# Tokenizer and first attention of a vision tower: the order of all engines written by hand

## The chip, the cores and the metric

The kernel runs on one core of one Trainium2 chip. The metric is the device time of one execution in microseconds (us). A core has a matrix engine (TensorE, PE in the profile), three engines for elementwise work (VectorE or DVE, ScalarE or ACT, GpSimd or POOL), and SyncE (SP), whose queue issues most of the transfers. Each engine has a queue of its own, and the engines wait for each other through semaphores.

## The reference

32 images of 3 x 256 x 256 become 256 tokens of width 256 each, and pass two layers. All arithmetic is in float32. The part that the change touches is the tokenizer, the first attention and the start of the first FFN:

```
h = patches @ W.T + b                                 # tokenizer
xn = layernorm(h) / max(norm(layernorm(h)) / 16, 1e-5) * g
uv = silu(xn @ W_uv + b_uv)                           # u 512, v 512, base 128 columns
q, k = base * gamma[0] + beta[0], base * gamma[1] + beta[1]
attn = square(relu(q @ k.T / sqrt(128)))
h = h + (u * (attn @ v)) @ W_o + b_o
y = layernorm(h);  weights = y @ wr + br              # FFN: the best 127 of 256 tokens of an image
sel = the 127 tokens of greatest weight
h = h + y;  h[sel] += weights[sel] * (gelu(sel @ w1 + b1) @ w2 + b2)
```

The second layer (an attention by phases, and a gated FFN with heads and experts) is computed after that and is not changed in its order.

## The kernel before, in words

The residual `H` stays on chip for all 32 images: two chunks of 128 tokens by 256 columns each. The work goes in stages: A, the tokenizer, one image at a time; B, the first attention, two images (a pair) at a time; C, the FFN with token choice, four images (a quad) at a time; then the second layer. Line numbers are those of the kernel before unless said otherwise. All matmuls are recorded by the helper `mm` (L114), transposes by their own lines (L187 for activations, L349 for weights of tokens, L240 for chosen tokens), the add of an image's patches by L303, statistics by `stats` (L122 and L123), the normalisation by `normed` (L173).

**Stage A**, `unit_a`: for each image 12 matmuls of 128 x 256 from patches that SP loads up to five images ahead, one add of the bias into `H` on VectorE, and the statistics of both chunks. After each second image `factors_b` makes the scale of the next normalisation: four small operations on GpSimd (two powers among them) and two on VectorE (L327, L328). PE, ACT and SP follow the written order here, VectorE and GpSimd an order that the scheduler chose.

**Stage B**, `unit_b`, in a pipeline of pairs, in whose newest stage a pair is normed (`bx`, L173), turned (`transposed`: eight transposes into two banks, of which ACT copies the first at L192 and VectorE the second at L194), and its `base` is made (two matmuls of 128 x 512, Silu on ACT at L392) with queries and keys `bq`, `bk` on VectorE (L394, L396). A step later the pair has its scores with relu (ACT, L405) and square (GpSimd, L407), its gates `uT` (eight matmuls, L415) and its values `bv` (eight matmuls, an add on VectorE at L422, Silu on ACT at L423). Another step later come the products of attention and values, gated on VectorE into `gT` (L439), and the output with `w_wo`, whose result VectorE adds to `H` (L452) before it takes the statistics for stage C and GpSimd makes their power. `b_o` is added to `H` by GpSimd (L382).

Two further steps belong to stage C: `norm_c` norms the images of the pair (`cx`) and makes the weights of tokens `cw` (L341, with a sum as a second result); `ranks` calls `rank_c` for both images. `rank_c` has two transposes of `cw` into half of a bank which both images share, then four comparisons on VectorE (L354 and L356, twice each), three small operations, and two indirect stores on GpSimd (L365), which write the normed tokens to memory in their order of rank. In stage B the scheduler orders all engines: `phase` only says in which order the parts are handed to it.

**Stage C** is in written order on all engines already. It begins with the ranks of the last two pairs, and then has hidden layer, output and fetch of each quad. The second layer is ordered by the scheduler.

Of the kernel before, what the change touches and what calls it, by code (L numbers as in the profile page):

```python
# [32 lines left out]
F32 = mybir.dt.float32  # L33
# [6 lines left out]
P = 128  # L40
# [38 lines left out]
def vit_tower(tc, a, out):  # L79
# [115 lines left out]

    def one_step(active):
        return [g for g in active if next(g, g) is not g]

    def phase(unit, images, steps):

        active = []
        for b in range(0, B, images):
            active = one_step([unit(b)] + active)
        for _ in range(steps - 1):
            active = one_step(active)
        return active


    region, passing_x = ExitStack(), ExitStack()
# [33 lines left out]

    patches = a["patches"].rearrange("(k p) t -> p k t", p=P)
    with (
        tc.tile_pool(name="a_w", bufs=1) as pw,
        tc.tile_pool(name="a_x", bufs=6) as pp,  # L250
        tc.manual_schedule(engines={ENG.PE, ENG.Activation, ENG.SP}),
    ):
# [33 lines left out]

        loaded = []
        st_b = new_stats("b")

        def unit_a(b):  # L290
            if b == 0:
                ps = [bank() for _ in range(NC)]
                for k in range(n_k):
                    for c in range(NC):
                        mm(ps[c][:, 0:D], x0[k][:, c * P : (c + 1) * P], tokW[k], k == 0, k == n_k - 1)
                for c in range(NC):
                    nc.vector.tensor_tensor(H[b][:, c, :], ps[c][:, 0:D], row_a("tok_b"), ALU.add)
            else:
                x, p = xs_a.pop(b), bank()
                for c in range(NC):  # L300
                    for k in range(n_k):
                        mm(p[:, c * D : (c + 1) * D], x[:, k, c * P : (c + 1) * P], tokW[k], k == 0, k == n_k - 1)
                nc.vector.tensor_tensor(  # L303
                    H[b], p.rearrange("p (c d) -> p c d", c=NC), over(row_a("tok_b"), [P, NC, D], 1), ALU.add
                )
                if b + 5 < B:
                    load_patches(b + 5)
            st, _, i = at(st_b, b)
            for c in range(NC):
                stats(st, i, c, H[b][:, c, :])  # L310
            if b == 4:
                loaded.extend(layer_0_weights())
            if b % 2:
                factors_b(b - 1)
            yield

        def factors_b(b):


            st, rs, i = at(st_b, b)  # L320
            q = slice(i * NC, (i + 2) * NC)
            var = st.rearrange("p i c s -> p (i c) s")[:, q, 1]
            low = spool.tile([P, 2 * NC], F32, name="low")
            pow_rstd(low, var)
            nc.gpsimd.tensor_scalar(rs[:, q], var, 1e-36, 1.0, ALU.max, ALU.mult)
            nc.gpsimd.tensor_tensor(rs[:, q], rs[:, q], minus_half[:, 0 : 2 * NC], ALU.pow)
            nc.vector.scalar_tensor_tensor(rs[:, q], low, 1e5, rs[:, q], ALU.mult, ALU.min)  # L327
            nc.vector.tensor_scalar(rs[:, q], rs[:, q], col("attn_g"), None, ALU.mult)  # L328

        phase(unit_a, 1, 2)  # L330
        wuv, row_b, wo, row_c, before, w1 = loaded

    def norm_c(b):
        x = px.tile([P, NC, D], F32, name="cx", bufs=6)
        normed(x, b, st_c)
# [33 lines left out]
    with (  # L369
# [3 lines left out]
        st_c = new_stats("c")  # L373
        scale = 1.0 / math.sqrt(128.0)

        def unit_b(b0):
            xs = []
            for j in range(2):
                x = p4.tile([P, NC, D], F32, name="bx")
                normed(x, b0 + j, st_b)  # L380
                xs.append(x)
                nc.gpsimd.tensor_tensor(  # L382
                    H[b0 + j], H[b0 + j], over(row_b("b_o"), [P, NC, D], 1), ALU.add
                )
            xT = p2.tile([P, 2, 2 * N], F32, name="bxT")
            transposed(xT, xs, copy_split)

            base = p2.tile([P, 2 * N], F32, name="base")
            p = bank()
            for k in range(2):  # L390
                mm(p, wuv[:, k, 1024:1152], xT[:, k, :], k == 0, k == 1)
            nc.scalar.activation(base, p, AF.Silu, bias=col("b_base"))  # L392
            q = p2.tile([P, 2 * N], F32, name="bq")
            nc.vector.tensor_scalar(q, base, col("gamma", 0), col("beta", 0), ALU.mult, ALU.add)  # L394
            kk = p2.tile([P, 2 * N], F32, name="bk")
            nc.vector.tensor_scalar(kk, base, col("gamma", 1), col("beta", 1), ALU.mult, ALU.add)  # L396

            yield
            attn = []
            for j in range(2):  # L400
                p = bank()
                for m in range(NC):
                    mm(p[:, m * N : (m + 1) * N], kk[:, j * N + m * P : j * N + (m + 1) * P], q[:, j * N : (j + 1) * N])
                r = p2.tile([P, NC, N], F32, name="relu")
                nc.scalar.activation(r.rearrange("p m n -> p (m n)"), p, AF.Relu, scale=scale)  # L405
                t = p4.tile([P, NC, N], F32, name="attn")
                nc.gpsimd.tensor_tensor(t, r, r, ALU.mult)  # L407
                attn.append(t)

            uT = p2.tile([P, 4, 2 * N], F32, name="uT")  # L410
            for hc in range(4):
                p = bank()
                for k in range(2):
                    mm(p, wuv[:, k, hc * P : (hc + 1) * P], xT[:, k, :], k == 0, k == 1)
                nc.scalar.activation(uT[:, hc, :], p, AF.Silu, bias=col("b_u", hc))  # L415
            vs = []
            for tb in range(2 * NC):
                p = bank()
                for k in range(2):
                    mm(p, xT[:, k, tb * P : (tb + 1) * P], wuv[:, k, 512:1024], k == 0, k == 1)  # L420
                v = p4.tile([P, 512], F32, name="bv", bufs=8)
                nc.vector.tensor_tensor(v, p, row_b("b_v"), ALU.add)  # L422
                nc.scalar.activation(v, v, AF.Silu)  # L423
                vs.append(v)

            yield
            gTs = []
            for j in range(2):
                gT = p2.tile([P, 4, N], F32, name="gT")
                for half in range(2):  # L430
                    p = bank()
                    for h in range(2):
                        hc = 2 * half + h
                        for m in range(NC):
                            mm(
                                p[:, h * N : (h + 1) * N], vs[j * NC + m][:, hc * P : (hc + 1) * P],
                                attn[j][:, m, :], m == 0, m == NC - 1,
                            )
                    nc.vector.tensor_tensor(  # L439
                        gT[:, 2 * half : 2 * half + 2, :], p.rearrange("p (h n) -> p h n", h=2),  # L440
                        uT[:, 2 * half : 2 * half + 2, j * N : (j + 1) * N], ALU.mult,
                    )
                gTs.append(gT)
            if b0 == B - 2:
                turn_c(0, quads[0], 0)
            for j in range(2):
                b, gT = b0 + j, gTs[j]
                p = bank()
# [5 lines left out]
                for c in range(NC):  # L454
                    stats(st, i, c, H[b][:, c, :])

            pow_rstd_of(st_c, b0, 2)

            yield
            normed_c[b0] = [norm_c(b0 + j) for j in range(2)]  # L460

            yield
            ranks(b0)
            if b0 in (2, 6):
                first_ranks(b0 - 2, quads[b0 // 4], 0)

# [6 lines left out]


        phase(unit_b, 2, 3)
    region_b.close()

# [211 lines left out]
    with region_c:  # L689
# [20 lines left out]
        def fetch(b0, s, half):  # L710
            s.y = s.y if half else []
            for b in range(b0 + 2 * half, b0 + 2 * half + 2):
                y = px.tile([P, NC, D], F32, name="cx", bufs=6)
                for c in range(NC):
# [31 lines left out]
        preparing = prepare()  # L746
        with tc.manual_schedule(engines={ENG.PE, ENG.DVE, ENG.Activation, ENG.Pool, ENG.SP}):
            for t in range(END_C):
                if t < 2:
                    ranks(B - 4 + 2 * t)  # L750
                if t == 0:
                    normed_c[B - 2] = [norm_c(B - 2 + j) for j in range(2)]
                if t == END_C - 2:
                    norm_d(0, pairs[0], px, "cx", 6)
                step_c(t)
                if t >= 8:
                    next(preparing, None)
        passing.close()
    region.close()
    region_c0.close()  # L760


    st_e = new_stats("e")
    with (
# [45 lines left out]
        def values_d(b0, s):  # L810
            s.v = []
            for j in range(2):
                p = bank()
                for c in range(NC):
                    for k in range(2):
                        o = j * N + c * P
                        mm(p[:, c * D : (c + 1) * D], s.xT[:, k, o : o + P], wv[:, k, :], k == 0, k == 1)
                v = p8.tile([P, NC, D], F32, name="dv", bufs=6)
                nc.vector.tensor_tensor(
# [783 lines left out]
```

## Time and profile before

| | us |
|---|---|
| median of three runs | 2049.75 |
| lowest and highest run | 2048.95 and 2054.02 |
| the profiled execution, its own time | 2053.58 |
| span of the profiled execution | 2051.8 |
| end of stage A on TensorE in it (from the span's start) | 173.04 |
| end of the last output matmuls of stage B | 711.89 |

The profile has six parts: busy time of each engine, the span in 40 slices, the DMA queues, the chain of work that ended last, the costliest groups of instructions, and the transfers. Each row of the timeline is an instruction or several equal ones with their start, their length, and, in brackets, how long their engine sat idle before them and what ended that. A float32 matmul shows as two rows. The granted clock of TensorE stands in windows as a number from 0 to 1; its mean over the span is 0.977.

### The profile page before, as it was taken

What the parts mean: (1) busy time and instruction counts of PE and PEld (TensorE: products, weight loads), DVE (VectorE), ACT (ScalarE), POOL (GpSimd) and SP (SyncE); (2) the same over time, 40 slices, a digit from 0 to 9 for tenths busy, and PEclk for the clock granted to TensorE, in tenths of its full rate; (3) what the DMA queues carried; (4) which work ended last, traced back from release to release, by engine and by line L of the source; (5) the groups of instructions that cost most, each with busy time, mean ns of one, the idle gap of its engine ahead of it and who ended that gap; (6) DMA issues with size and microseconds to landing.
All of it is one profiled execution on the core that took longest, in us unless ns stands there. A gap on an engine that the chain in (4) does not pass through costs nothing.

```text
span 2051.8 us, 38271 instructions
## 1 busy us (share of the span) xinstructions
PE 1973.4 (96%) x15412; PEld 1431.7 (70%) x15412; DVE 1334.2 (65%) x3591; ACT 832.5 (41%) x1569; POOL 731.1 (36%) x691
## 2 busy tenths in 40 slices
PE   9998999999999899999999999999999999999983
PEld 8885676666667657666667677667777777777762
DVE  2335557667675634435655566547898989998986
ACT  0001322222221121222443444367777777777762
POOL 1224224334341443336432333103444444444443
PEclk9999999999999999999998999989999999999996
DMA  9540000000000222221000000001121212121212
GB/s 296 151 135 1 0 1 31 18 24 16 16 18 29 87 81 72 60 70 57 1 0 1 1 1 1 1 17 38 39 63 43 64 43 63 44 62 45 64 48 53
DMA packets 69687, 95.12 MB, mean 46 GB/s; under 512 B 8576, under 2 KB 50944, under 8 KB 69120
## 3 DMA queue, kind: packets, MB, share of 16 engines
q1 hardware_dynamic: 62784, 75.04, 13.1%
q0 software_dynamic: 6144, 16.79, 2.7%
q8 instruction: 123, 2.02, 0.4%
q10 hardware_dynamic: 576, 0.79, 0.1%
q14 instruction: 60, 0.49, 0.1%
HBM read 46.45 MB, written 20.97 MB: 33 GB/s over the span
## 4 chain that ended last, share of the span: by engine, by line
PE 90%; DVE 5%; DMA 1%; ACT 1%; issue 1%; POOL 1%; SPq 0%; DVEq 0%; ACTq 0%; POOLq 0%
PE bank L114 85%; PE bank L646 2%; PE bank L187 2%; PE bank L1148 1%; DMA both<-hx 1%; PE bank L349 1%; DVE bank L994 0%; ACT bxT L192 0%; DVE fout L1157 0%; PE bank L240 0%; DMA patch<-in_patches_dram 0%; DMA cx<-results,rank_of 0%; DVE six L122 0%; DVE two L1079 0%; DVE fout L1153 0%
## 5 line engine op out<-in xcount | busy, mean ns | idle before, releaser
L996 ACT ACTIVATE et<-bank 128x512 f32<-128x512 f32 x384 | 202.4, 598 | 59.0 <-DVE bank L994 58.3
L114 PEld LDWEIGHTS bank<-ev,et 128*64 128x64 f32 x6144 | 198.0, 137 | 33.8 <-ACT et L996 21.3
L994 DVE TENSOR_TENSOR bank<-bank,w_tri 128x256 f32<-128x256 f32 (+1 forms) x384 | 173.6, 514 | 69.6 <-PE bank L114 67.6
L114 PE MATMUL bank<-ev,et 128*64 128x74 f32 (+1 forms) x6144 | 210.9, 226 | 0.0
L1074 POOL TENSOR_TENSOR eo<-eo,gate 128x1024 f32<-128x1024 f32 x64 | 121.9, 1925 | 226.5 <-DVE gate L1071 207.9
L114 PE MATMUL bank<-g,sx 64*128 64x512 f32 (+1 forms) x512 | 192.7, 506 | 0.7 <-ACT g L954 0.7
L114 PE MATMUL bank<-g,sw 64*128 64x512 f32 (+1 forms) x512 | 191.8, 506 | 0.0
L114 PE MATMUL bank<-tokW,patch 128*128 128x256 f32 x768 | 166.7, 380 | 2.3 <-DMA patch<-in_patches_dram 2.3
L114 PEld LDWEIGHTS bank<-tokW,patch 128*128 128x128 f32 x768 | 146.1, 190 | 23.0 <-issue 2.7
L114 PE MATMUL bank<-bxT,w_wuv 128*128 128x512 f32 x320 | 149.2, 605 | 5.5 <-ACT bxT L192 3.9
L192 ACT COPY bxT<-bank 128x512 f32<-128x512 f32 x16 | 9.4, 586 | 342.6 <-PE bank L187 342.6
L1026 POOL TENSOR_TENSOR hv<-hv,minus_half 128x8 f32<-128x8 f32 x64 | 119.5, 1867 | 5.3
L1012 ACT COPY eo<-bank 128x286 f32<-128x286 f32 x256 | 97.2, 421 | 58.3 <-PE bank L114 51.8
L114 PE MATMUL bank<-xsel,w_w 128*128 128x512 f32 x256 | 113.3, 600 | 0.0
L114 PE MATMUL bank<-attn,bv 128*128 128x256 f32 x512 | 113.3, 379 | 0.0
L114 PE MATMUL bank<-w_wo,gT 128*128 128x256 f32 x512 | 113.1, 379 | 0.0
L114 PE MATMUL bank<-w_w,hT 128*128 128x256 f32 x512 | 113.1, 379 | 0.0
L114 PE MATMUL bank<-w_wuv,bxT 128*128 128x512 f32 x256 | 112.5, 592 | 0.0
L114 PEld LDWEIGHTS bank<-attn,bv 128*128 128x128 f32 x512 | 97.1, 190 | 19.5 <-issue 6.9
L114 PEld LDWEIGHTS bank<-w_w,hT 128*128 128x128 f32 x512 | 96.7, 190 | 15.8 <-issue 3.3
L114 PEld LDWEIGHTS bank<-w_wo,gT 128*128 128x128 f32 x512 | 97.2, 190 | 13.2
L114 PEld LDWEIGHTS bank<-bxT,w_wuv 128*128 128x128 f32 x320 | 59.8, 192 | 66.3 <-issue 53.0
(245 smaller groups left out, 3980.2 us busy)
## 6 DMA issues: line engine op xcount, KB each, us to landing
patch<-in_patches_dram SPq DMA_DIRECT2D x31, 768.0 KB, 4.7
sw<-sx SPq DMA_DIRECT2D x64, 128.0 KB, 2.4
both<-fxT SPq DMA_DIRECT2D x64, 128.0 KB, 2.5
both<-hx SPq DMA_DIRECT2D x64, 128.0 KB, 2.3
out_dram<-fout SPq DMA_DIRECT2D x32, 256.0 KB, 2.5
cs<-ranked SPq DMA_DIRECT2D x32, 128.0 KB, 3.0
results<-cy SPq DMA_DIRECT2D x32, 128.0 KB, 1.7
w_w<-in_w_dram SPq DMA_DIRECT2D x2, 1024.0 KB, 10.2
```

The lines of the kernel that those rows point to most:

```text
L114: nc.tensor.matmul(o, lhsT, rhs, start=first, stop=last)
L187: nc.tensor.transpose(p[:, o : o + P], x[:, c, k * P : (k + 1) * P], ident)
L192: nc.scalar.copy(o, i)
L349: nc.tensor.transpose(pw[:, c * P : (c + 1) * P], w[:, c : c + 1].to_broadcast([P, P]), ident)
L646: nc.tensor.transpose(p[:, o : o + P], x[:, c, k * P : (k + 1) * P], ident)
L994: nc.vector.tensor_tensor(own, own, over(tri, [P, n_e, P], 1), ALU.add)
L996: nc.scalar.activation(t, p, AF.Exp)
L1012: nc.scalar.copy(im.o[:, c * NH + n, 0:OC], p[:, 0:OC])
L1026: nc.gpsimd.tensor_tensor(v, v, minus_half, ALU.pow)
L1074: nc.gpsimd.tensor_tensor(im.mix[k], im.mix[k], over(im.gate[:, :, 2 * k : 2 * k + 2], [P, NC * NH, 2, HD], 3), ALU.mult)
L1148: nc.tensor.transpose(im.po[:, o : o + P], im.fT[:, k, c * P : (c + 1) * P], ident)
```

## The change

From the start of stage A to the end of stage C one block, `by_hand`, now keeps the written order on PE, VectorE, ACT, GpSimd and SP; after it the scheduler works as before. The generators `unit_b` and `phase` are gone. Their parts are functions (`norm_b`, `turn_b`, `base_b`, `queries_b`, `scores_b`, `gates_b`, `values_b`, `gated_b`, `output_b`), which a loop over steps t calls in a written order. `ranks` stands between base and queries; the norm of the next pair is the last call of a step.

In stage A `factors_b` is split: `powers_b` on GpSimd after the odd image, the two operations on VectorE an image later. Pairs 0 and 1 are normed after images 26 and 28. Pair 0 is turned, and has its base, queries and keys, ahead of the last image; these lie in tiles (`xsel`, `cs`) of stage C which are not yet in use. Normed tokens of stage B now come from the pool `cx`, with 8 buffers where there were 6. `dv`, a tile of the second layer, has 4 buffers instead of 6.

```diff
-        tc.manual_schedule(engines={ENG.PE, ENG.Activation, ENG.SP}),
+    by_hand = ExitStack()
+    by_hand.enter_context(tc.manual_schedule(engines={ENG.PE, ENG.DVE, ENG.Activation, ENG.Pool, ENG.SP}))
...
+    def norm_b(b0, s):
+        s.xs = []
+        for j in range(2):
+            x = px.tile([P, NC, D], F32, name="cx", bufs=8)
+            normed(x, b0 + j, st_b)
+            s.xs.append(x)
+            h = H[b0 + j]
+            nc.gpsimd.tensor_tensor(h, h, over(row_b("b_o"), [P, NC, D], 1), ALU.add)
...
-        phase(unit_a, 1, 2)
+        for b in range(B):
+            if b == B - 1:
+                half = [p0.tile([P, 4, D], F32, name="cs", bufs=2).rearrange("p j d -> p (j d)") for _ in range(2)]
+                turn_b(0, pairs_b[0], p0, "xsel")
+                base_b(0, pairs_b[0], half[0][:, 0 : 2 * N])
+                queries_b(0, pairs_b[0], half[0][:, 2 * N :], half[1][:, 0 : 2 * N])
+            unit_a(b)
+            if b == 4:
+                wuv, row_b, wo, row_c, before, w1 = layer_0_weights()
+            if b % 2:
+                powers = powers_b(b - 1)
+            elif b:
+                factors_b(*powers)
+            if b in (B - 6, B - 4):
+                u = (b - B + 6) // 2
+                norm_b(2 * u, pairs_b[u])
...
-        phase(unit_b, 2, 3)
+        for t in range(B // 2 + 2):
+            def pair(u):
+                return (2 * u, pairs_b[u]) if 0 <= u < B // 2 else None
+
+            new, old, older = pair(t) if t else None, pair(t - 1), pair(t - 2)
+            if new:
+                turn_b(*new, p2, "bxT")
+                base_b(*new, p2.tile([P, 2 * N], F32, name="base"))
+            if t >= 4:
+                ranks(2 * (t - 4))
+                if t in (5, 7):
+                    first_ranks(2 * t - 10, quads[t // 2 - 2], 0)
+            if new:
+                queries_b(*new, p2.tile([P, 2 * N], F32, name="bq"), p2.tile([P, 2 * N], F32, name="bk"))
+            if old:
+                scores_b(*old)
+                gates_b(*old)
+                values_b(*old)
+            if t == 1:
+                factors_b(*powers)
+            if t >= 3:
+                normed_c[2 * (t - 3)] = [norm_c(2 * (t - 3) + j) for j in range(2)]
+            if older:
+                gated_b(*older)
+                if t == B // 2 + 1:
+                    turn_c(0, quads[0], 0)
+                output_b(*older)
+            if 2 <= t + 1 < B // 2:
+                norm_b(*pair(t + 1))
...
-                v = p8.tile([P, NC, D], F32, name="dv", bufs=6)
+                v = p8.tile([P, NC, D], F32, name="dv", bufs=4)
```

The other functions of the list hold the statements of `unit_b` unchanged.

More of the change, by code (lines that the diff above doesn't have):

```diff
@@ L194, in copy_split @@
             nc.vector.tensor_copy(o, i)
[L196 to L209, printed above, removed]
+    by_hand = ExitStack()
+    by_hand.enter_context(tc.manual_schedule(engines={ENG.PE, ENG.DVE, ENG.Activation, ENG.Pool, ENG.SP}))
     region, passing_x = ExitStack(), ExitStack()
@@ L247, in vit_tower, with turn_b, base_b, queries_b @@
     patches = a["patches"].rearrange("(k p) t -> p k t", p=P)
+    st_b, st_c = new_stats("b"), None
+    scale = 1.0 / math.sqrt(128.0)
+    class PairB:
+        pass
+    pairs_b = [PairB() for _ in range(B // 2)]
+    def norm_b(b0, s):
[6 more added lines that the diff above has]
+            nc.gpsimd.tensor_tensor(h, h, over(row_b("b_o"), [P, NC, D], 1), ALU.add)
+    def turn_b(b0, s, pool, name):
+        s.xT = pool.tile([P, 2, 2 * N], F32, name=name)
+        transposed(s.xT, s.xs, copy_split)
+    def base_b(b0, s, base):
+        s.base, p = base, bank()
+        for k in range(2):
+            mm(p, wuv[:, k, 1024:1152], s.xT[:, k, :], k == 0, k == 1)
+        nc.scalar.activation(base, p, AF.Silu, bias=col("b_base"))
+    def queries_b(b0, s, q, k):
+        s.q, s.k = q, k
+        nc.vector.tensor_scalar(q, s.base, col("gamma", 0), col("beta", 0), ALU.mult, ALU.add)
+        nc.vector.tensor_scalar(k, s.base, col("gamma", 1), col("beta", 1), ALU.mult, ALU.add)
     with (
@@ L285, in layer_0_weights @@
             )
-        loaded = []
-        st_b = new_stats("b")
         def unit_a(b):
@@ L310, in unit_a, with powers_b @@
                 stats(st, i, c, H[b][:, c, :])
[L311 to L317, printed above, removed]
+        def powers_b(b):
             st, rs, i = at(st_b, b)
@@ L326, in factors_b @@
             nc.gpsimd.tensor_tensor(rs[:, q], rs[:, q], minus_half[:, 0 : 2 * NC], ALU.pow)
-            nc.vector.scalar_tensor_tensor(rs[:, q], low, 1e5, rs[:, q], ALU.mult, ALU.min)
-            nc.vector.tensor_scalar(rs[:, q], rs[:, q], col("attn_g"), None, ALU.mult)
-        phase(unit_a, 1, 2)
-        wuv, row_b, wo, row_c, before, w1 = loaded
+            return rs[:, q], low
+        def factors_b(rs, low):
+            nc.vector.scalar_tensor_tensor(rs, low, 1e5, rs, ALU.mult, ALU.min)
+            nc.vector.tensor_scalar(rs, rs, col("attn_g"), None, ALU.mult)
+        for b in range(B):
[14 more added lines that the diff above has]
+                norm_b(2 * u, pairs_b[u])
     def norm_c(b):
-        x = px.tile([P, NC, D], F32, name="cx", bufs=6)
+        x = px.tile([P, NC, D], F32, name="cx", bufs=8)
         normed(x, b, st_c)
@@ L373, in vit_tower, with scores_b @@
         st_c = new_stats("c")
[L374 to L399, printed above, removed]
+        def scores_b(b0, s):
+            s.attn = []
             for j in range(2):
@@ L402, in unit_b @@
                 for m in range(NC):
-                    mm(p[:, m * N : (m + 1) * N], kk[:, j * N + m * P : j * N + (m + 1) * P], q[:, j * N : (j + 1) * N])
+                    o = j * N + m * P
+                    mm(p[:, m * N : (m + 1) * N], s.k[:, o : o + P], s.q[:, j * N : (j + 1) * N])
                 r = p2.tile([P, NC, N], F32, name="relu")
@@ L407, in unit_b, with gates_b @@
                 nc.gpsimd.tensor_tensor(t, r, r, ALU.mult)
-                attn.append(t)
-            uT = p2.tile([P, 4, 2 * N], F32, name="uT")
+                s.attn.append(t)
+        def gates_b(b0, s):
+            s.uT = p2.tile([P, 4, 2 * N], F32, name="uT")
             for hc in range(4):
@@ L413, in unit_b, with values_b @@
                 for k in range(2):
-                    mm(p, wuv[:, k, hc * P : (hc + 1) * P], xT[:, k, :], k == 0, k == 1)
-                nc.scalar.activation(uT[:, hc, :], p, AF.Silu, bias=col("b_u", hc))
-            vs = []
+                    mm(p, wuv[:, k, hc * P : (hc + 1) * P], s.xT[:, k, :], k == 0, k == 1)
+                nc.scalar.activation(s.uT[:, hc, :], p, AF.Silu, bias=col("b_u", hc))
+        def values_b(b0, s):
+            s.vs = []
             for tb in range(2 * NC):
@@ L419, in unit_b @@
                 for k in range(2):
-                    mm(p, xT[:, k, tb * P : (tb + 1) * P], wuv[:, k, 512:1024], k == 0, k == 1)
+                    mm(p, s.xT[:, k, tb * P : (tb + 1) * P], wuv[:, k, 512:1024], k == 0, k == 1)
                 v = p4.tile([P, 512], F32, name="bv", bufs=8)
@@ L423, in unit_b, with gated_b @@
                 nc.scalar.activation(v, v, AF.Silu)
-                vs.append(v)
-            yield
-            gTs = []
+                s.vs.append(v)
+        def gated_b(b0, s):
+            s.gTs = []
             for j in range(2):
@@ L435, in unit_b @@
                             mm(
-                                p[:, h * N : (h + 1) * N], vs[j * NC + m][:, hc * P : (hc + 1) * P],
-                                attn[j][:, m, :], m == 0, m == NC - 1,
+                                p[:, h * N : (h + 1) * N], s.vs[j * NC + m][:, hc * P : (hc + 1) * P],
+                                s.attn[j][:, m, :], m == 0, m == NC - 1,
                             )
@@ L440, in unit_b, with output_b @@
                         gT[:, 2 * half : 2 * half + 2, :], p.rearrange("p (h n) -> p h n", h=2),
-                        uT[:, 2 * half : 2 * half + 2, j * N : (j + 1) * N], ALU.mult,
+                        s.uT[:, 2 * half : 2 * half + 2, j * N : (j + 1) * N], ALU.mult,
                     )
-                gTs.append(gT)
-            if b0 == B - 2:
-                turn_c(0, quads[0], 0)
+                s.gTs.append(gT)
+        def output_b(b0, s):
             for j in range(2):
-                b, gT = b0 + j, gTs[j]
+                b, gT = b0 + j, s.gTs[j]
                 p = bank()
@@ L457, in unit_b @@
             pow_rstd_of(st_c, b0, 2)
[L459 to L465, printed above, removed]
         normed_c = {}
@@ L712, in fetch @@
             for b in range(b0 + 2 * half, b0 + 2 * half + 2):
-                y = px.tile([P, NC, D], F32, name="cx", bufs=6)
+                y = px.tile([P, NC, D], F32, name="cx", bufs=8)
                 for c in range(NC):
@@ L746, in vit_tower @@
         preparing = prepare()
[L747 to L757, printed above, removed]
+        for t in range(END_C):
+            if t < 2:
+                ranks(B - 4 + 2 * t)
+            if t == 0:
+                normed_c[B - 2] = [norm_c(B - 2 + j) for j in range(2)]
+            if t == END_C - 2:
+                norm_d(0, pairs[0], px, "cx", 8)
+            step_c(t)
+            if t >= 8:
+                next(preparing, None)
         passing.close()
@@ L760, in vit_tower @@
     region_c0.close()
+    by_hand.close()
     st_e = new_stats("e")
```

## The prediction

> **What bounds the kernel now.** I read the page first: busy shares and the chain that ended last.
>
> ```profile
> PE 1973.4 (96%) x15412; PEld 1431.7 (70%) x15412; DVE 1334.2 (65%) x3591; ACT 832.5 (41%) x1569; POOL 731.1 (36%) x691
> PE 90%; DVE 5%; DMA 1%; ACT 1%; issue 1%; POOL 1%; SPq 0%; DVEq 0%; ACTq 0%; POOLq 0%
> ```
>
> TensorE is the bound: 90% of the chain is its own work. The change can only win where TensorE idles, and loses wherever it makes TensorE wait. So I cut the time at the stage borders (columns: stretch, its length, busy us of PE, PEld, DVE, ACT, POOL, then the granted clock, DMA share, GB/s).
>
> ```profile
> 173.04:204.32 31.28, 25.73 (x64) 12.19 (x65) 19.19 (x32) 9.55 (x14) 15.66 (x14) 0.84 0.00 1
> 204.32:665.10 460.78, 457.01 (x1670) 302.54 (x1669) 293.50 (x718) 108.53 (x169) 158.58 (x148) 1.00 0.05 17
> 665.10:721.02 55.92, 47.04 (x193) 34.38 (x192) 39.66 (x129) 8.33 (x12) 22.64 (x25) 0.94 0.27 86
> ```
>
> The join from tokenizer to attention (first row) wastes TensorE at a clock of 0.84. The attention's steady part has 3.8 us of idle in 461 us at full clock: nothing is to be had there. The third row is the join to the FFN, which the change touches only at its edge. Next, one steady step on TensorE in the timeline (start, us, and the wait before it in brackets).
>
> ```profile
> 532.87 0.38 PE L349 MATMUL bank<-ident,cw 128*128 128x128 f32 x2
> 533.09 1.04 PE L187 MATMUL bank<-ident,bx 128*128 128x128 f32 x8
> 534.37 1.13 PE L114 MATMUL bank<-bxT,w_wuv 128*128 128x512 f32 x2 [0.24 <-ACT bxT L192]
> 535.33 1.46 PE L114 MATMUL bank<-bq,bk 128*128 128x256 f32 x6
> 536.62 1.02 PE L114 MATMUL bank<-bxT,w_wuv 128*128 128x512 f32 x2
> 537.68 0.43 PE L349 MATMUL bank<-ident,cw 128*128 128x128 f32 x2
> 565.93 0.38 PE L349 MATMUL bank<-ident,cw 128*128 128x128 f32 x2
> ```
>
> The step is 565.93 - 532.87 = 33.06 us. The scheduler put score matmuls (bq,bk) between the two base matmuls, and 4.6 us between the rank transposes of one image and of the other (L349): each wait for VectorE is filled with other matmuls.
>
> [...] Both images of a pair share one rank bank, so the second image's transposes wait until VectorE has read the first's; the trace has that wait at 2.15 to 4.46 us (below). [...] half clock for 10.2 us from 714.8 and 3.4 us from 977.7. [...] four norms took 1.41 us, but three beside a GpSimd add took 1.97.
>
> **The join A to B: a gain.** Before, TensorE went 31.28 us from the tokenizer's end to the next turn. Its work in there, at full-clock pitches: two turns of 8 transposes (16 x 0.109 = 1.7), four base matmuls of two rows (8 x 0.43 = 3.4), scores (8 x 0.216 = 1.7), gates and values (32 x 0.43 = 13.7): 20.6 us. Wasted: 10.7. After, pair 0 was normed at images 26 and 28, and its turn and base stand ahead of image 31. Waits that stay: ACT's copy of the first half (0.45); VectorE's copy of the second, queued behind image 30's add, statistics and factors (about 1.1); for pair 1, again 0.45, and 0.6 for its copy behind image 31's statistics. Sum 2.6. Gain 10.7 - 2.6 = 8.1, its slow clock included. The rest of the tokenizer is free: an image takes 5.2 us on TensorE, VectorE needs some 2.6 of it plus 1.4 for norms at two images, and the GpSimd powers (2.5) get a whole image's time.
>
> **The turn: a new wait, once a step.** In the changed program as built, VectorE's order at the end of a step is: add of the second image's output, its statistics, four norms of the *next* pair, and TensorE goes from the last output matmul straight to the transposes of those norms. Nothing is queued between them; behind the waiting transpose stand all matmuls of the next step. Count from X, the end of TensorE's issue of the output. Rows:
>
> ```profile
> 562.68 0.69 DVE L452 TENSOR_TENSOR h<-h,bank 128x512 f32<-128x512 f32 x1 [2.76 <-PE bank L114]
> 955.02 0.43 DVE L122 BATCH_NORM_STATS2 six<-h 128x6 f32<-128x256 f32 x1
> 955.48 0.18 DVE L123 BATCH_NORM_AGGREGATE st_d<-six 128x2 f32<-128x6 f32 x1
> 961.03 1.41 DVE L173 TENSOR_SCALAR dx<-h,st_d,rs_d 128x256 f32<-128x256 f32 x4 [0.64 <-DMA results<-cy]
> ```
>
> VectorE starts its add at X+0.20 (566.13 against 565.93 before). Add to statistics 0.73; two times (0.46 to the aggregate, 0.10 on): free at X+2.05. Norms 1.41: X+3.46. Fourth transpose 0.15 later, X+3.6; ACT copies from X+3.97 to 4.56, base starts X+4.6; VectorE's copy is done at about 5.2, before the second half needs it at 5.5; four rows of 0.43 end at X+6.33. GpSimd's `b_o` add stands behind its two rstd operations (0.2 and 1.04 us after the statistics), so it starts when the norms are nearly over and I give them no contention; if it hits, up to 1.0 more.
>
> **The ranks: a second wait in the same step.** They now come right after base, four transposes in a row; the second two wait for VectorE's four comparisons.
>
> ```profile
> 715.39 0.69 PE L349 MATMUL bank<-ident,cw 128*128 128x128 f32 x2 [2.90 <-DVE ctmp L356]
> 720.54 0.69 PE L349 MATMUL bank<-ident,cw 128*128 128x128 f32 x2 [4.46 <-DVE ctmp L356]
> 729.89 0.38 PE L349 MATMUL bank<-ident,cw 128*128 128x128 f32 x2
> 732.43 0.43 PE L349 MATMUL bank<-ident,cw 128*128 128x128 f32 x2 [2.15 <-DVE ctmp L356]
> ```
>
> The last pair is the clean case, VectorE being free: 732.43 - 729.89 = 2.54, and 0.27 to the next matmul. So the second image's transposes start at X+6.33+2.54 = 8.87 and scores at X+9.14. Scores 1.73, gates 6.87, values 6.87, gated 6.9, output 6.9 bring the step to 38.4 us: 5.35 over 33.06. The rest of the step stays covered: VectorE's norm_c (3.5 to 4.6 us, behind the last value add) ends before the output matmuls need its first product, with 1 us to spare. GpSimd's four indirect stores now wait for the ranks and hold back the squares (attn), but these are used a step later. Twelve steps (t=4 to 15) have both waits: 12 x 5.35 = 64.2. Step 3 has the turn alone: base ends at 6.33 instead of 2.6, less the 0.4 of before: +3.3. Step 2, behind the value adds and factors: +2.6. Steps 16 and 17 have ranks right behind the output: VectorE free at 2.05, comparisons to 4.1: 4.0 each, against 1.4 and 0.1 before: +6.5. The FFN join had 711.89 to 721.02 with 0.9 us of transposes: 8.2 wasted; one such wait (4.0) remains, and 16 rows at half clock cost 9.04 instead of 7.03: -6.2.
>
> **The clock.** Granted clock is the number after the POOL column:
>
> ```profile
> 714.00:716.00 2.00, 0.61 (x2) 0.29 (x2) 1.60 (x9) 0.00 (x0) 1.57 (x4) 0.70 0.92 310
> 722.00:724.00 2.00, 2.00 (x4) 0.87 (x3) 1.89 (x10) 0.00 (x0) 0.73 (x2) 0.50 0.51 181
> 730.00:732.00 2.00, 0.27 (x3) 0.03 (x1) 1.58 (x5) 0.69 (x1) 2.00 (x2) 1.00 0.19 66
> ```
>
> Three sparse stretches (174, 713, 973 us) halved the clock; extra time of the matmuls within: about 2.8, 2.0 and 1.4, mean 2.0. A lone 2.15 us gap at 730 did not. The new step has two sparse stretches within 9 us (0 to 3.6, and 6.5 to 8.9). Bounds per step: 0, and 4.0 (both halve it). I take 1.2 stretches, 2.4 us: 12 x 2.4 = 28.8; the five single ones at 1.8: 9.
>
> The other edits go at nothing: cx from 6 to 8 buffers holds the norms; `dv` from 6 to 4 still holds two pairs, and on all engines the order from layer 1's attention on is that of before; the SP queue has the same 280 rows.
>
> **Sum.** -8.1 + 64.2 + 3.3 + 2.6 + 6.5 - 6.2 + 28.8 + 9 = +100. The profiled execution took 2053.58 (span 2051.8, 1.8 around it): 2153.7, and its span 2152. The median shown is 3.8 lower: 2150.
>
> **Rivals.** *The clock stays full* [...]: 100 - 38 = +62, 2112. Against: 30% activity sufficed for the fall at 714.8. *The clock recovers late*, 10.2 us each as at 714.8, or GpSimd slows the norms: 12 x 2.6 more, 2181. *The norms are ready in time* and only the ranks wait (14 x 2.3, a clock loss of 1 each, less 8.1): 2088. Against: norms stand behind the statistics. *Faster*: one mechanism, the join. Its 8.1 us decide if the 28 new waits (14 turns, 14 ranks) come under 0.3 us each, that is if VectorE runs a step ahead of TensorE: 2042. Speaks for it: VectorE is only 65% busy. Against: its add needs the last output matmul. *The change does nothing*: the built order differs in every step, so very unlikely.
>
> **Chances.** Forecast (2125 to 2170) 0.60; clock full 0.14; clock late 0.13; ranks only 0.08; faster 0.03; no change 0.02. The range 2108 to 2174 takes the first two and little of the third. Within 0.3% (6 us) is what a measurement of this kernel can't tell from no change. Slower 0.95, same 0.02, faster 0.03.
>
> **What would show it.** Right: 9 to 10 us between the last output matmul and the scores in each step; waits of the transposes (L187) for the norms and of the rank transposes for the comparisons, some 2 us each, 14 and 15 times; step 39 to 42 us; clock 0.5 in places of every step; A to B join about 23 us. Wrong: a step near 33 us, or norms dated before the statistics.

## The result and the profile after

| | before | after |
|---|---|---|
| median of the runs compared, us | 2049.35 (four runs, 2046.16 to 2054.02) | 2154.05 (four runs, 2147.33 to 2158.98) |
| the profiled execution, own time (span) | 2053.58 (2051.8) | 2158.98 (2157.1) |
| mean granted clock in it | 0.977 | 0.957 |
| mean step of pairs, t = 4 to 15 | 33.00 | 41.07 |

The changed kernel is slower: ratio 1.051, interval 1.047 to 1.055. The forecast was 2150, in a range of 2108 to 2174.

Of the page after, the busy shares and the chain that ended last:

```profile
PE 2027.1 (94%) x15412; PEld 1463.3 (68%) x15412; DVE 1318.3 (61%) x3591; ACT 832.2 (39%) x1569; POOL 730.1 (34%) x691
PE 90%; DVE 6%; DMA 1%; ACT 1%; issue 1%; POOL 0%; SPq 0%; DVEq 0%; ACTq 0%; POOLq 0%
```

TensorE has as many instructions as before and is busy 54 us longer. Since the count is the same, they ran at a lower clock or their records hold time in which they stood. The other 52 us of the 105 are idle time. The chain hardly shows it: VectorE has 6% of it where it had 5%.

The stretches of time, cut as before at the stage borders (length, busy us of PE, PEld, DVE, ACT and POOL, granted clock, DMA share, GB/s):

```profile
173.53:198.00 24.47, 23.86 (x77) 13.53 (x75) 6.49 (x13) 7.79 (x12) 4.55 (x6) 1.00 0.00 0
198.00:764.40 566.40, 507.74 (x1673) 329.22 (x1673) 285.63 (x746) 108.88 (x169) 167.05 (x156) 0.92 0.04 14
```

The first row runs from the start of the last image to the end of the first values, now at full clock with 0.6 us of idle; the stretch behind the tokenizer had 5.6 before. The second is the attention's steady part: it took 460.78 us with 3.8 of idle at a clock of 1.00, and now takes 566.40 with 58.7 of idle at 0.92. That is the loss, and the rest of the kernel isn't needed to explain it.

One steady step of the changed kernel in TensorE's timeline (start, us, and in brackets the idle time before and what ended it):

```profile
480.14 2.30 PE L187 MATMUL bank<-ident,cx 128*128 128x128 f32 x8 [2.30 <-DVE cx L173]
482.26 2.79 PE L114 MATMUL bank<-bxT,w_wuv 128*128 128x512 f32 x4
484.89 0.38 PE L379 MATMUL bank<-ident,cw 128*128 128x128 f32 x2
487.43 0.69 PE L379 MATMUL bank<-ident,cw 128*128 128x128 f32 x2 [2.15 <-DVE ctmp L386]
487.91 3.30 PE L114 MATMUL bank<-bq,bk 128*128 128x256 f32 x8
...
521.10 2.30 PE L187 MATMUL bank<-ident,cx 128*128 128x128 f32 x8 [2.30 <-DVE cx L173]
```

The step is 521.10 - 480.14 = 40.96 us. Nothing stands any more between the transposes of norms and the output matmuls ahead of them, or between the rank transposes of the two images: two idle times, 2.30 and 2.15 us, where the step before had one of 0.24. The durations carry a second sign. Eight score matmuls take 3.30 us; at full clock they take 1.89 (e5 below has such a row; in a step before they came as six, 1.46 us, and two, 0.60). Both waits come in every step; this is TensorE's list of waits from 300 to 757 us (us in total, times, longest):

```profile
PE bank L187 <- DVE cx L173: 25.3, 11, 2.3
PE bank L379 <- DVE ctmp L386: 23.7, 11, 2.2
```

There is no third line. Nothing else waits in this stretch, neither for the gated products behind norm_c nor for the squares.

The clock in one step, in windows of 2 us (it is the number after the POOL column):

```profile
522.60:524.60 2.00, 2.00 (x6) 1.24 (x5) 0.69 (x1) 0.57 (x1) 2.00 (x2) 0.50 0.00 0
524.60:526.60 2.00, 1.64 (x5) 0.47 (x3) 0.33 (x1) 0.55 (x1) 0.14 (x1) 0.93 0.00 0
...
528.60:530.60 2.00, 2.00 (x7) 1.64 (x7) 1.48 (x6) 0.00 (x0) 1.06 (x1) 0.50 0.09 31
```

It falls to half twice in the step, once after each wait. Last the two joins. From tokenizer to attention:

```profile
169.51 1.04 PE L187 MATMUL bank<-ident,cx 128*128 128x128 f32 x8
...
191.04 7.03 PE L114 MATMUL bank<-w_wuv,xsel 128*128 128x512 f32 x16
```

The values end some 6.87 us after the last of these starts, at 197.9. From 169.51 to there are 28.4 us, and 5.2 of them are the last image. And to the FFN:

```profile
821.47 0.38 PE L379 MATMUL bank<-ident,cw 128*128 128x128 f32 x2
...
826.05 8.34 PE L114 MATMUL bank<-xsel,w_w 128*128 128x512 f32 x16
```

The hidden layer starts 4.58 us after the last output; before, it was 9.13.

### The profile page after: what moved, and what is told of

Read it like the earlier page. It is cut to its first block, busy times and chain, and to the rows that moved or that the text cites. A ratio compares the mean times of both kernels' runs of the same rounds, so it can differ in the third digit from the quotient of the medians.

```text
span 2157.1 us, 38268 instructions
## 1 busy us (share of the span) xinstructions
PE 2027.1 (94%) x15412; PEld 1463.3 (68%) x15412; DVE 1318.3 (61%) x3591; ACT 832.2 (39%) x1569; POOL 730.1 (34%) x691
## 4 chain that ended last, share of the span: by engine, by line
PE 90%; DVE 6%; DMA 1%; ACT 1%; issue 1%; POOL 0%; SPq 0%; DVEq 0%; ACTq 0%; POOLq 0%
PE bank L114 83%; PE bank L187 3%; PE bank L677 2%; DVE six L122 1%; DVE ctmp L386 1%; PE bank L1179 1%; DVE ctmp L384 1%; DMA both<-hx 1%; PE bank L379 1%; DVE h L463 1%; DVE cx L173 0%; DMA cx<-results,rank_of 0%; DMA patch<-in_patches_dram 0%; PE bank L228 0%; DVE fout L1188 0%
## 5 line engine op out<-in xcount | busy, mean ns | idle before, releaser
L433 DVE TENSOR_TENSOR bv<-bank,rows_b 128x512 f32<-128x512 f32 x64 | 44.3, 692 | 187.0 <-PE bank L114 187.0
L395 POOL DMA_INDIRECT ranked<-cx,rank_to x64 | 66.0, 1031 | 119.9 <-DMA ranked<-cx,rank_to 62.2
```

The lines of the kernel that those rows point to most:

```text
L395: nc.gpsimd.indirect_dma_start(ranked[b][:], bass.IndirectOffsetOnAxis(rank_to[:, k : k + 1], 0), x[:, c, :], None)
```

## The experiments

All start from the changed kernel and are compared with runs of the kernel before on the same chip (medians 2050.5, 2047.9 and 2050.6 us in the three batches). "Step" is the mean of t = 4 to 15, from one start of the output matmuls to that twelve steps later.

| run | edit | median us | ratio to before, interval | step us |
|---|---|---|---|---|
| before | | 2049.35 | 1 | 33.00 |
| changed kernel | | 2154.05 | 1.051 (1.047 to 1.055) | 41.07 |
| e1_norm_early | next pair normed after the queries | 2098.91 | 1.024 (1.021 to 1.027) | 37.36 |
| e2_two_banks | a rank bank for each image | 2101.46 | 1.025 (1.022 to 1.028) | 37.59 |
| e3_both | both edits | 2041.08 | 0.995 (0.994 to 0.996) | 33.45 |
| e5_filler | unread matmuls in both waits | 2113.11 | 1.031 (1.028 to 1.034) | 38.38 |
| e7_early_filler | e1, unread matmuls in the ranks' wait | 2077.45 | 1.014 (1.011 to 1.017) | 35.82 |
| e4_sched_b | scheduler orders stage B | 2052.15 | 1.001 (1.000 to 1.002) | 34.05 |
| e6_scores_first | e3, scores between turn and base | 2023.20 | 0.985 (0.983 to 0.988) | 32.35 |
| e8_pair_after | e6, pair 0 turned after the last image | 2022.59 | 0.987 (0.984 to 0.990) | 32.35 |

**Each wait taken away alone, then both.** e1 moves one call, so that VectorE has the norms of the next pair done long before the turn:

```diff
                 queries_b(*new, p2.tile([P, 2 * N], F32, name="bq"), p2.tile([P, 2 * N], F32, name="bk"))
+            if 2 <= t + 1 < B // 2:
+                norm_b(*pair(t + 1))
             if old:
...
                 output_b(*older)
-            if 2 <= t + 1 < B // 2:
-                norm_b(*pair(t + 1))
```

> The changed kernel with one edit: the norm of the next pair is called after the queries of a step and not after its output. Theory (the turn waits for norms that stand behind the output's statistics, the ranks for comparisons on a shared bank, and both sparse stretches halve TensorE's clock): the turn's wait is gone, steps 2 and 3 fall to 33 us, steps 4 to 15 to 35.5 to 37 (one wait of 2.15 us stays, with the clock mostly full); about 2075, range 2065 to 2095. Rival A (what costs is the hand order on GpSimd and VectorE as a whole, or the shared pool of normed tokens): the norms' place matters little, 2130 or more. Rival B (the clock loss hangs on the ranks' gap alone): about 2105.

e2 gives each image of a pair its own rank bank and issues all four transposes ahead of the comparisons:

```diff
         def ranks(b0):
-            pw = bank()
+            pws = [bank()[:, 0:N] for j in range(2)]
+            for j in range(2):
+                spread_c(normed_c[b0][j][1], pws[j])
             for j in range(2):
-                rank_c(b0 + j, *normed_c[b0][j], pw[:, j * N : (j + 1) * N])
+                rank_c(b0 + j, *normed_c[b0][j], pws[j])
```

(`spread_c` is the two transposes, taken out of `rank_c`.)

> The changed kernel with one edit: each image of a pair gets a rank bank of its own, and the four transposes are issued before any comparison. Theory: TensorE no longer waits for comparisons, in steps 4 to 17 and at the start of the FFN; the turn's wait stays. Step 38 to 39 us (33.06 + 3.3 + about 2 of slow clock); total about 2105, range 2090 to 2118. Rival A (the comparisons are needed in time by something else, so the wait moves on to the queries or the indirect stores): 2140 or more. Rival B (the clock loss hangs on the turn's gap alone, and stays whole): about 2118.

e3 has both edits.

> The changed kernel with both edits: norms after the queries, and two rank banks. Theory: no wait longer than 0.6 us is left in stage B, the clock stays full there, step 33.0 us; the gains at both joins stay (6.4 and about 9 us): about 2033, range 2026 to 2042, faster than the kernel before. Rival A (hand order as such costs): 2060 or more. Rival B (gains of the joins are not there, only the waits were): 2049.

Measured: 2098.91, 2101.46 and 2041.08. With neither wait the whole loss is gone (the kernel is 0.5% faster than before); with one of them half of it is left. So the loss comes from these two waits and what they bring, and the rest of the change is a small gain. e2 also shows that the wait at the ranks was for the shared bank, since TensorE has the four transposes in the same order with one bank and with two. With two banks the wait of 2.15 us is gone from every step: e2's list of TensorE's waits has no line for the comparisons, and the changed kernel's has 39.1 us of them in 16 waits.

e1 is a miss. It ended about 24 us above the centre of what was expected, and above the range too. The expectation held a single gap of 2.15 us to be too short for the clock. TensorE's timeline of e1 at the ranks shows otherwise:

```profile
491.07 0.38 PE L379 MATMUL bank<-ident,cw 128*128 128x128 f32 x2
493.61 0.43 PE L379 MATMUL bank<-ident,cw 128*128 128x128 f32 x2 [2.16 <-DVE ctmp L386]
493.88 3.25 PE L114 MATMUL bank<-bq,bk 128*128 128x256 f32 x8
```

The eight score matmuls after the lone gap take 3.25 us instead of 1.89. The mean clock of its steps (300 to 705 us) is 0.95.

e3 ended at the upper end of what was expected: its step is 33.45, not 33.0. Its list of waits has two small ones in each step, 0.24 us for ACT's copy of the first half of the turn and 0.32 for VectorE's of the second, with nothing in between. Before, score matmuls covered the second. Against the kernel before, e3 gains nothing in the steps, which are 0.45 us longer; its profile has the gains at the two joins.

**Wait and clock taken apart.** e5 keeps both waits but fills them with matmuls whose result nobody reads, five of 128 x 256 ahead of the turn and five between the rank transposes of the two images. TensorE then stays busy without being any earlier: in a step of e5 the turn starts 2.47 us after the output's issue and the second rank transposes 2.53 us after the first, as in the changed kernel (2.47 and 2.54).

```diff
             if new:
+                if t >= 2:
+                    filler(5)
                 turn_b(*new, p2, "bxT")
...
             for j in range(2):
+                if j and b0 < B - 4:
+                    filler(5)
                 rank_c(b0 + j, *normed_c[b0][j], pw[:, j * N : (j + 1) * N])
```

> The changed kernel with work added: five matmuls of 128 x 256 (2.16 us at full clock), whose result nobody reads, ahead of each turn from step 2 on and between the rank transposes of the two images in steps 4 to 17. Both waits stay as they are; TensorE is only kept busy in them. Theory (2.7 us a step of the loss is slow clock, which the idle stretches cause): the clock stays at 1.00 in stage B and a step falls from 41.0 to about 38.4 although it holds more work; total about 2120, range 2112 to 2130. Rival (the slow clock costs nothing of its own, since it falls into waits): no gain, 2154, or up to 2165 where the fillers come too late.

A step of e5 in TensorE's timeline; the fillers are the rows with `w_wuv,ident`:

```profile
459.72 2.32 PE L114 MATMUL bank<-w_wuv,ident 128*128 128x256 f32 x10
462.19 1.74 PE L187 MATMUL bank<-ident,cx 128*128 128x128 f32 x8
...
466.20 2.32 PE L114 MATMUL bank<-w_wuv,ident 128*128 128x256 f32 x10
...
468.78 1.89 PE L114 MATMUL bank<-bq,bk 128*128 128x256 f32 x8
```

The kernel with more work is 41 us faster than the changed kernel: 2113.11 against 2154.05. Its scores take 1.89 us again and its clock is 1.00 from 300 to 683 us. The step is 38.38. So the waits alone cost 38.38 - 33.00 = 5.38 us in a step, and the clock 41.07 - 38.38 = 2.69.

e7 puts the same filler into e1's single wait, to see whether the lone gap really cost e1 its clock. Its edit is that of e1 and the second half of e5's.

> The changed kernel with early norms and one shared rank bank (as the run with the norm early), with five unread matmuls of 128 x 256 between the rank transposes of the two images. The wait itself stays. Theory (a lone wait of 2.15 us does halve the clock where it falls badly: the step of 37.5 us in the run with the norm early is 33.46 + 2.15 + 1.9 of slow clock): clock 1.00 in stage B, step 35.6; 12 steps and the two steps after them give 2099 - 26 = about 2073, range 2067 to 2080. Rival (the 1.9 us is another wait, as a bank or the queries that come late): step stays 37.5 and the time 2099.

The step falls from 37.36 to 35.82 and the clock is 1.00 (300 to 684 us). The lone gap does halve the clock; that explains e1's miss. But it does so in eleven of the twelve steps only. The first of them took 35.81 us in e1, as with the filler, the others 37.50 each, so a halving cost 1.69 (half a window of the clock, below, is 1.71). What tells the first gap from the next one is in e1's own trace. In the profiles of the kernel before and of the changed kernel the granted clock changes only on a grid of 3.413 us (all 17 changes of the one and all 71 of the other), and these are four windows of e1's grid (columns as above):

```profile
265.56:268.97 3.41, 2.22 (x6) 0.62 (x5) 1.90 (x6) 0.69 (x1) 1.21 (x2) 1.00 0.00 0
268.97:272.38 3.41, 2.12 (x11) 1.91 (x12) 3.00 (x13) 0.60 (x1) 1.21 (x1) 1.00 0.03 7
...
303.10:306.51 3.41, 1.26 (x7) 0.70 (x6) 2.25 (x9) 0.69 (x1) 0.26 (x1) 1.00 0.00 0
306.51:309.92 3.41, 3.41 (x10) 2.72 (x9) 3.23 (x12) 0.62 (x2) 1.42 (x2) 0.50 0.13 43
```

The first gap, from 268.11 to 270.26 us, is shared by two windows; TensorE is busy for more than 2.1 us of each, and the clock stays full. The second, from 303.93 to 306.08, lies inside one window, which leaves 1.26 us of work, and the next window has half the clock. The gap at 730 us of the kernel before was shared too: 1.81 us busy in the window from 728.46 and 2.86 in the next.

**The scheduler in stage B, the rest of the change kept.** e4 was meant to show the change's other parts alone:

```diff
+    by_hand.close()
     with (
         tc.tile_pool(name="b_2", bufs=2, reuse_waits="tile") as p2,
...
+    by_hand.enter_context(tc.manual_schedule(engines={ENG.PE, ENG.DVE, ENG.Activation, ENG.Pool, ENG.SP}))
     region_b.close()
```

> The changed kernel with its hand order lifted for stage B alone: stage A keeps it, with pair 0 turned ahead of the last image, and stage C too, but the calls of stage B are handed to the scheduler as before. Theory (the join of A to B is a gain of its own, and only the hand order in B costs): step 33 us as before, the join keeps its 6 to 8 us; about 2044, range 2039 to 2049. Rival A (the join's gain is undone when the scheduler takes over, or hides in a later wait): 2050, no difference. Rival B (what costs is something else in the change, as the shared pool of normed tokens or the 4 buffers of the values in layer 1): above 2060.

It ended at 2052.15, not measurably different from before, where a gain was expected. It is no clean test of that. Once the scheduler held VectorE, it put eight norms of later pairs ahead of the add of image 30, and a copy of the turned pair 0 came late in the join (TensorE's timeline of e4):

```profile
175.77 2.08 PE L114 MATMUL bank<-xsel,w_wuv 128*128 128x512 f32 x2 [3.53 <-DVE xsel L194]
```

Its steps are longer than before as well, 34.05: of the 19.0 us of waits at the shared rank bank that are left in this kernel, each step has about 1. What it shows is only that the scheduler, given the same calls, doesn't make the two long waits that the written order has.

**A better written order.** e6 takes e3 and puts the scores of the older pair, which wait for nothing, between the turn and its base:

```diff
                 turn_b(*new, p2, "bxT")
+            if old:
+                scores_b(*old)
+            if new:
                 base_b(*new, p2.tile([P, 2 * N], F32, name="base"))
...
             if old:
-                scores_b(*old)
                 gates_b(*old)
```

> The changed kernel with early norms and two rank banks (as the run with both), and the scores of the older pair called between turn and base, so that they fill the wait for the two copies of the turn. Theory (each step of the run with both still loses 0.56 us to these copies, 33.46 against 33.06): step 32.8 to 32.95, 15 steps, about 8 us less than the run with both: 2033, range 2028 to 2038. Rival (TensorE is at its own pace by then, or the relu of the scores delays base and queries): 2041, as the run with both.

A step of e6 in TensorE's timeline:

```profile
454.47 1.04 PE L187 MATMUL bank<-ident,cx 128*128 128x128 f32 x8
455.34 1.89 PE L114 MATMUL bank<-bq,bk 128*128 128x256 f32 x8
457.07 1.88 PE L114 MATMUL bank<-bxT,w_wuv 128*128 128x512 f32 x4
458.79 0.60 PE L379 MATMUL bank<-ident,cw 128*128 128x128 f32 x4
459.22 7.03 PE L114 MATMUL bank<-bxT,w_wuv 128*128 128x512 f32 x16
```

No row has a bracket, and this stretch of e6 (columns as above) shows TensorE without a break:

```profile
198.00:640.00 442.00, 442.00 (x1624) 293.65 (x1623) 276.35 (x728) 108.23 (x169) 162.13 (x154) 1.00 0.05 17
```

At 2023.20 us it beats both kernels: ratio 0.985 (0.983 to 0.988) to before. It did better than expected (2028 to 2038). The expectation counted the 0.56 us of idle time in e3's step, but a wait costs more than the idle time of its row: in e3 the first base matmul starts 1.28 us after the turn (466.88 to 468.16 in its trace), in e6 the scores start 0.87 after it, 0.41 sooner for a wait of 0.24. Against the kernel before, the step is 0.65 us shorter: turn, base, scores and ranks of a step take 459.22 - 454.47 = 4.75 us in one piece, and 5.51 before (499.82 to 505.33 in its trace), broken into smaller pieces with a wait of 0.24 among them.

**Pair 0 after the last image.** e8 is e6 with the turn, base and queries of pair 0 put back behind the tokenizer:

```diff
         for b in range(B):
-            if b == B - 1:
-                half = [p0.tile([P, 4, D], F32, name="cs", bufs=2).rearrange("p j d -> p (j d)") for _ in range(2)]
-                turn_b(0, pairs_b[0], p0, "xsel")
-                base_b(0, pairs_b[0], half[0][:, 0 : 2 * N])
-                queries_b(0, pairs_b[0], half[0][:, 2 * N :], half[1][:, 0 : 2 * N])
             unit_a(b)
...
+        half = [p0.tile([P, 4, D], F32, name="cs", bufs=2).rearrange("p j d -> p (j d)") for _ in range(2)]
+        turn_b(0, pairs_b[0], p0, "xsel")
+        base_b(0, pairs_b[0], half[0][:, 0 : 2 * N])
+        queries_b(0, pairs_b[0], half[0][:, 2 * N :], half[1][:, 0 : 2 * N])
```

> The run with the scores first, with one part of the change undone: pair 0 is turned, and has its base, queries and keys, after the last image and not ahead of it (its norms stay at image 26). Theory (most of the join's gain comes from the early norms and the written order, since the scheduler had put norms and powers of other pairs ahead; turning pair 0 early only hides the way from base over ScalarE and VectorE to the scores): from the end of the last image to the scores some 2 to 3 us more of TensorE's waits than with pair 0 ahead, about 2025, in the trace rather than in the median. Rival (turning pair 0 ahead is the gain): the join loses the 8 us again, 2031.

The medians, 2022.59 and 2023.20, can't be told apart. In the traces the join of e8 has idle times of 0.24, 0.33 and 1.03 us, 1.6 in all, and that of e6 has 0.24 and 0.66, 0.9 in all. The turn ahead of the last image saves 0.7 us of waits, where 2 to 3 were expected. This holds for e6's order, in which the scores of an older pair stand between turn and base; in the changed kernel's own order it was not tried.

## Why the prediction was right, point by point

The forecast of 2150 stands beside 2154.05, and the mechanism is the one described: two new waits for VectorE in every step, and the clock after them. By the terms of its sum, with profiled times:

| term | predicted us | measured us |
|---|---|---|
| join from tokenizer to attention | -8.1 | -6.4 |
| waits of steps 4 to 15 | +64.2 | +64.6 (12 x 5.38) |
| clock in steps 4 to 15 | +28.8 | +32.3 (12 x 2.69) |
| steps 2 and 3 with their clock | +9.5 | +8.9 |
| steps 16 and 17 with their clock | +10.1 | +10.3 |
| join to the FFN with its clock | -4.4 | -5.3 |
| the rest | 0 | +1 |
| sum | +100 | +105.4 |

The measured terms come from starts of rows in the two timelines. For example, steps 2 and 3 last 66.8 us from the end of the first values to the output group of t = 3 and lasted 57.9 before. The division of steps 4 to 15 into wait and clock is e5's.

- **The turn and the ranks: right.** The prediction counted from the end of the output's issue, X, and had the second image's rank transposes at X + 8.87 and the scores at X + 9.14. In e5, where the clock stays full, X is 459.72, and the scores are at X + 9.06. In the changed kernel, at half clock in part, they come 10.2 us after X (487.91, with X 6.95 us after the start of the output at 470.72, as in e5). The durations from single rows of the kernel before (add, statistics, four norms, comparisons) were enough, since nothing else is in VectorE's queue there.
- **Norms not slowed by GpSimd: right.** Four norms took 1.37 us in the changed kernel's step (1.41 assumed). GpSimd's add of `b_o` began at 522.26, after VectorE's norms had ended at 522.02. In the tokenizer the two did meet: there the four norms took 2.33 us (161.47 to 163.80, GpSimd's add from 162.28), not 1.4, in time that VectorE had to spare.
- **The clock: right in sum, wrong in its parts.** The prediction took 1.2 halvings in a step at 2.0 us each, because the gap of 2.15 us at 730 us of the kernel before had not halved the clock. Each step has two, and they cost 2.69 together, 1.34 each. The step that failed is the reading that "a lone 2.15 us gap did not", taken as a rule from one place: e1 and e7 show that a lone gap of the same length costs 1.69 us where it falls inside one window of the clock, in eleven of e1's twelve steps, and nothing where two windows share it, as at 730 us (1.60 and 0.55 us) and in e1's first step (0.86 and 1.29). Two errors nearly cancelled, 1.2 for 2 and 2.0 for 1.34; that the sum came within 3.5 us is luck. The rival in which the clock stays full would have given 2112. That is what e5 measures (2113.11), with matmuls added to keep it full.
- **The join from tokenizer to attention: size right, reason only in part.** From the turn to the end of the values it takes 28.4 - 5.2 = 23.2 us, the predicted 20.6 + 2.6, and took 31.28. In the profiled execution 1.7 us of the 8.1 are lost again, since TensorE came to this point at 169.5, not 167.9, after a lower clock in the first 15 us (0.89 up to 12 us and 0.85 up to 15, where the kernel before has 1.00). That point lies between 167.6 and 171.6 us in the profiles of the changed kernel and of the experiments with the same order up to there, so I don't put this down to the change. The prediction gave the gain to the early norms and the early turn together. e8 gives less than 1 us of it to the turn, in e6's order; so most comes from what e8 keeps: norms made during the last images, and the written order of VectorE. These two were not tried apart.
- **Steps 16 and 17 and the FFN join: right.** Each was given 4.0 us of waste at the ranks behind the output. In all three places it takes some 4.6 us from the first rank transpose to the next other matmul, and 0.44 of that is work (four transposes of 0.109).
- **The free edits: right.** No wait in the steps is for a gated product, a square or a buffer.
- **The rival with the opposite sign** (VectorE runs ahead of TensorE, so that only the join counts) was rightly held unlikely for this order. It is what e3 builds: moving the norms away from the end of the step and giving the ranks two banks takes away what made TensorE wait. It was put at 2042, and e3 took 2041.08, but that the numbers agree is luck: the rival counted the first join alone, while e3's twelve steps are 5.4 us longer than before, and it has 6.9 us back at the join to the FFN (9.13 us from the last output's start to the hidden layer, 707.84 to 716.97 in its trace, and 16.04 before). The rival with the ranks' wait alone was put at 2088, with 1 us of clock for each; e1 builds it and took 2098.91, at 1.69 each.

Where the expected gain went, then: it came in at the joins, and was lost many times over in the steps, where the scheduler had already found what the written order left out, other matmuls between a result of TensorE and the matmul that needs VectorE's answer to it.

One thing is open: how much work a window needs. Windows that were idle in part were enough for a fall. It was so in the kernel before too: the window ahead of the fall at 714.81 us has TensorE busy for 32%. A count of its busy time in the profiles of both kernels over all windows at full clock shows the rest. All 38 windows with less than 40% were followed by half clock, and none of the 1097 with 61% or more. Of the 13 between, 7 were, so there the busy share alone doesn't decide: e1's gap at 782.58 us left a window with 47%, and the clock stayed, while the changed kernel's turn at 274.07 us, whose gap of 2.29 us has 1.77 in one window, left a window with 48%, all of it transposes, and it fell.

In the changed kernel and in e2 the steps settled on whole windows: from 41.57 to 40.96 us, and from 37.70 to 37.55, which are 12.00 and 11.00 of them. So each gap keeps its place in a window and costs in every step, where a single gap costs or not by where it falls. In e1 the steps of 37.50 us are 0.05 short of eleven windows: its gap moves ahead by that much a step, from 0.83 to 0.39 us behind the start of its window, and stayed inside it. No run shows why the two others settle.

## What to carry to other kernels

When an order is written by hand, look at every place where a matmul needs an answer of another engine to the matmul just before it, and put matmuls there that need nothing: make the next step's operand early in this step, and give results that are read one after the other banks of their own. A wait of some 2 us in a steady loop has to be priced with the clock as well, here at half of its length again (2.69 us beside 5.38 in a step); that a single gap elsewhere in the same trace left the clock alone is no measure: look whether it lay inside one of the windows on whose borders the clock changes, here 3.413 us long, and whether the loop's step is near a whole number of them, as here with 12.00 and 11.00, so that its gap lies there every time. And before a hand order replaces a scheduler's, read in the timeline which matmuls it had put into which gaps, and keep them.

## What the runs showed of the hardware that was not expected

- Filling idle time of TensorE with matmuls that nobody reads made the kernel faster: 2113.11 us against 2154.05, all of it by the clock, since the waits are as long (2.47 and 2.53 us, and 2.47 and 2.54).
- A lone idle time of 2.15 us halved the clock for 3.413 us where it lay inside one window of that length (eleven steps of e1, 37.50 us each, against 35.81 with the clock full) and not where two windows shared it (e1's first step, and 730 us of the kernel before).
- The clock changed only on a grid of 3.413 us (17 changes before, 71 in the changed kernel). At full clock, windows in which TensorE was busy for less than 40% were all followed by half clock (38 of 38 in these two profiles), those with 61% or more never (1097).
- Steps with two waits, and with the turn's alone, settled on 12.00 and 11.00 windows (40.96 and 37.55 us).
- The start differs between executions of the same instructions. In the first 16 us the clock fell to half for 0 us in e7, 3.4 in the changed kernel and 6.8 in e3, and the first turn started up to 4 us apart (167.6 in e7, 171.6 in e3).
